# Input statistics of a group normalisation taken in one pass about early group means, with other load sizes and another engine for the first scalings

## The chip, the core and the metric

The kernel runs on one NeuronCore of a Trainium2 chip. The metric is the device time of one execution in microseconds (us). The core has five engines that run their own instruction queues in order: PE (TensorE, matmul), DVE (VectorE), ACT (ScalarE), POOL (GpSimd) and SP (SyncE, which only issues transfers here). Transfers (DMAs) can be issued from the SP, ACT and POOL queues; all of them run on the core's 16 DMA engines.

## The reference, cut to what matters

The input `x` is float32, 384 channels of 192 x 192. Two layers follow each other; the change touches only the first normalisation.

```
x = x + attention(group_norm(x))     # layer 0
x = x + seven_convs(group_norm(x))   # layer 1: 13x13 and six dilated depthwise convolutions

group_norm: 32 groups of 12 channels, mean and variance over 12 x 192 x 192 values
attention:  qkv = W_qkv (1152 x 384) @ x;  2x2 max pooling;  3x3 depthwise convolution;
            8 heads of 48 channels, top-k softmax of q k^T over channels;
            GELU; each cell copied to 2x2; W_proj @ ...
```

The statistics of layer 0 have to be known before any value of `x` can be scaled, and so before the first product of `W_qkv` with scaled values. The whole input (56.6 MB) is therefore read once for the statistics and again, block by block, for the products.

## The kernel before

Channels lie on partitions, in three groups `j` = 0, 1, 2 of 128. The 192 rows are cut into `NB` = 24 blocks of 8 rows (`FB` = 1536 values per channel).

*The statistics stage* is written with an order by hand (`manual_schedule`): instructions stand on each engine in the order of the program text, and each engine works its queue in that order.

- Blocks B = 0 and 1 of all channels (the "rows") are loaded by `load` from SP as four half-blocks of 1,152 KB into the pool `ax`; they stay in memory for the main loop. The other 22 blocks of each `j` (`NX` = 22) are loaded by `load_blocks` one at a time, 768 KB each, in the order of the list `order`: all of j = 0, then 1, then 2 (66 blocks, numbered n). Eight of them (`kept`) stay for early products; the rest go through a ring of eight slots. The issuing queue is ACT for the first eight loads, then POOL for odd n and SP for even n. A slot is loaded again once the engine that read it is done.
- Each block is reduced either by DVE (three `bn_stats` of 512 values, L535) or, for the blocks named in `BY_ACT`, by ACT: two activations that sum (x - pivot) and its square (L531, L532). The pivots are means of what has been read of that channel.
- When a `j` is read, `aggregate` (L501, `bn_aggr`) joins the DVE results into a mean and variance per channel; sums from ACT are turned into the same form by small operations (L522 to L527). 128 channels aren't a whole number of groups of 12, so a few channels of the next `j` are read ahead (`spares`, L550 and L558).
- `group_stats` then joins channels to groups through PE in two passes: weighted means to group means (`mean_of`), group means back to channels, squared differences plus variances to group variances, an inverse square root, and scale and shift back to channels (L113 to L156). It runs for j = 0 (`ga`), j = 1 (`ge`) and j = 2 (`g`), spread between `bn_stats` by generators (`first_chunk`, `early`, `last`).
- Meanwhile PE begins the products that need only j = 0 (`first_chunk`) or j = 0 and 1 (`early`): 18 pieces (`EARLY`), named by block and by one of three output groups. ACT scales an input piece with `ready` (L418), PE multiplies (`multiply`, L429), ACT copies the product out of PSUM to memory (`put_by`, L440) and later back into PSUM (`fill`, L269), so that j = 2 can be added.
- POOL also merges the convolution weights (`merge`), sums 2x2 cells of scaled pieces for later (`sum_one`, L280 to L284) and zeroes buffers for the main loop (L633).

*The main loop* takes the 24 blocks twice, for q and k (12 steps a block) and for v (6 steps a block). A step is six matmul calls (`project`, L671), a 2x2 maximum on DVE (L683), a bias on ACT (L690) and 3x3 taps on DVE (L719). At the first step of block B the two half-blocks of B + 1 are loaded (`load`, L179, into four buffers); ACT scales them from the sixth step on in the first half, and from the third in the second (`normalize`, L651). `input_variance` (L962) works out the input's variance from the stored parts with one small DVE operation per step; it is used in layer 1.

The attention, the projection back (L1459) and layer 1's convolutions (L1371) follow.

Of the kernel before, what the change touches and what calls it, by code (L numbers as in the profile page):

```python
# [58 lines left out]
def tile_attn_then_large_kernel_conv(ctx: ExitStack, tc: tile.TileContext, a: dict, out: bass.AP):  # L59
# [112 lines left out]
    ax = ctx_x.enter_context(tc.tile_pool(name="ax", bufs=4, side="right"))  # L172
    xts = {}


    def load(B, sb):
        row0 = (B % NB * R + sb * SR) * 2
        xt = ax.tile([P, NJ, 2 * SR * W], F32, tag="xt", name=f"xt_{B}_{sb}")
        nc.sync.dma_start(  # L179
            out=xt,  # L180
            in_=x[:, row0 * W : (row0 + 2 * SR) * W].rearrange("(j p) n -> p j n", p=P),
        )
        xts[B, sb] = xt
# [5 lines left out]
    mvx = const.tile([P, 9, 2], F32, name="mvx")  # L189
    BY_ACT = ((4, 7, 10, 13, 16, 19), (4, 5, 7, 12, 15, 18), (0, 1))  # L190
    KINDS = ((0, 2), (0, 1, 2), (0, 2))
    PARTS = []
    terms = []
    for j in range(NJ):
        if j < 2:
            terms.append((len(terms), NJ + j))
        PARTS.append([])
        for q in KINDS[j]:
            share = (0, 1, len(BY_ACT[j]))[q] * R / HS
            if q == 0:  # L200
                share = 1 - (len(KINDS[j]) - 2 + len(BY_ACT[j])) * R / HS
            PARTS[j].append((len(terms), q, share))
            terms.append((len(terms), j))
# [23 lines left out]
    FB = R * 2 * W  # L227
    HB = FB // 2
# [62 lines left out]
    with (  # L291
# [9 lines left out]
        for B in range(2):  # L301
            for sb in range(2):
                load(B, sb)
        FX = NKEEP * FB
        NX = (HW - FX) // FB
        NS0 = 2 * 2 * 2
# [14 lines left out]
        xss, waiting = {}, list(range(NJ * NX))  # L321

        def load_blocks():

            while waiting:
# [9 lines left out]
                eng = nc.scalar if n < 8 else nc.gpsimd if n % 2 == 1 else nc.sync  # L335
                eng.dma_start(out=xs, in_=x[j * P : (j + 1) * P, FX + b * FB : FX + (b + 1) * FB])
# [13 lines left out]
        nc.gpsimd.dma_start(out=gm, in_=a["gm"].rearrange("(j p) g -> p j g", p=P))  # L350
        nc.gpsimd.dma_start(out=gmt[:, :C], in_=a["gmt"])
# [7 lines left out]
        gw = [s1.tile([P, NG], F32, name="gw")]  # L359
# [5 lines left out]
        o = NJ * HS * WS - 2 * SR * WS  # L365
        gw += [free[:, o - n * NG : o - (n - 1) * NG] for n in (1, 2)]
        assert len(gw) == len(terms)

        def merge():

            c0 = BC - 1
            for j in range(NJ):
# [12 lines left out]
                for jj in range(NJ):  # L385
                    for k, _, share in PARTS[jj]:
                        nc.gpsimd.tensor_scalar(gw[k], gm[:, jj], share, None, ALU.mult)
                    yield
                for jj in range(2):
# [4 lines left out]
                    k = P * (jj + 1) - 1  # L394
                    nc.gpsimd.tensor_copy(
                        gmt[:, C + jj * P : C + (jj + 1) * P], gmt[:, k : k + 1].to_broadcast([NG, P])
                    )
# [11 lines left out]
        def rows_stats(n):  # L409
            xt = xts[n // 2, n % 2]  # L410
            for j in range(NJ):
                nc.vector.bn_stats(stats[:, j, 2 * n, :], xt[:, j, :512])
                nc.vector.bn_stats(stats[:, j, 2 * n + 1, :], xt[:, j, 512:])

        def ready(B, sb, j):

            t = xts[B, sb][:, j] if B < NKEEP else kept[j, B - NKEEP][:, :HB]
            nc.scalar.activation(t, t, AF.Identity, bias=gn0[:, j, 1:2], scale=gn0[:, j, 0:1])  # L418
# [23 lines left out]
        def first_chunk():  # L442

            pc = yield from group_stats(s1, s_ps, mvx, "ga", gw, terms[: TWICE[1]], (0,), True)
            yield
            nc.vector.tensor_copy(gn0[:, 0], pc[:, 0])
            yield
            blocks = sorted({B for B, _ in EARLY if B >= NKEEP})
            ready(blocks[0], 0, 0)
# [15 lines left out]
        def early():  # L465
# [5 lines left out]
            for n, (B, m) in enumerate(EARLY):  # L471
# [13 lines left out]
                if n < NKEEP:  # L485
                    ready(n, 1, 1)
# [82 lines left out]
        for _ in range(4):  # L569
            next(last)  # L570
# [1045 lines left out]
```

## Time and profile before

| | us |
|---|---|
| four runs, median | 2866.99 (2863.77 to 2867.78) |
| the profiled execution | 2867.78 |
| its span, first to last instruction | 2866.0 |
| first early product on j = 0 (L429) | 81.48 |
| first early product on j = 1 (L429) | 123.92 |
| first main-loop matmul (L671) | 166.12 |

| engine | busy us | share of the span |
|---|---|---|
| PE | 2740.0 | 96% |
| DVE | 2498.1 | 87% |
| ACT | 1332.6 | 46% |
| POOL | 918.4 | 32% |

Times in a profile line count from the start of the span. In a timeline line they are the start, the duration, the engine, the line of the kernel, the operation, what it writes and reads, the number of instructions, and in brackets the idle time before it and what ended it. In a line of a windows view they are the stretch, its length, the busy time and instruction count of PE, of PE's weight loads, of DVE, ACT and POOL, then PE's granted clock, the DMA engines' share and GB/s. In a line of groups they are line, engine, operation, tiles, shapes and count, then busy us and mean ns of one, then idle time before and its releasers. Matmul ends are modelled, so times on PE are good to some tenths.

### The profile page before, as it was taken

The numbers are of one execution on the slowest core, as the hardware profiler recorded it, in microseconds if no ns is written. First come the engines' busy times: TensorE is split into PE (matmuls) and PEld (weight loads), VectorE is DVE, ScalarE is ACT, GpSimd is POOL, SyncE is SP. The second block draws the span as 40 slices with busy tenths as digits, with TensorE's granted clock in tenths as the row PEclk, the third lists the DMA queues.
The fourth block names the chain that finished last, engine by engine and source line by source line (L and its number), as shares of the span: only waits on it lengthen the run. The fifth ranks groups of instructions, "written<-read, shape, count | busy, mean of one in ns | idle before, by whom it ended". The sixth has DMA issues, their size and how long they took to land.

```text
span 2866.0 us, 37738 instructions
## 1 busy us (share of the span) xinstructions
PE 2740.0 (96%) x13662; PEld 1677.8 (59%) x13662; DVE 2498.1 (87%) x3484; ACT 1332.6 (46%) x2427; POOL 918.4 (32%) x1129
## 2 busy tenths in 40 slices
PE   0699999999999999999999999999999999999998
PEld 0356666666666666666655555545566666666666
DVE  6879997887878888788899988887789999999997
ACT  3755554444445444454444444444334444444443
POOL 4251231332323233231122222232115444445443
PEclk9899999999999999999999999999999999999999
DMA  9941432232423324242332333327889999999996
GB/s 389 419 149 64 134 120 80 86 121 72 135 74 101 102 71 135 67 135 79 102 111 96 113 118 114 118 65 223 233 202 286 261 273 273 271 278 270 256 270 174
DMA packets 269561, 475.75 MB, mean 166 GB/s; under 512 B 25858, under 2 KB 189968, under 8 KB 269248
## 3 DMA queue, kind: packets, MB, share of 16 engines
q1 hardware_dynamic: 204208, 301.51, 37.3%
q0 software_dynamic: 43328, 149.04, 15.6%
q10 hardware_dynamic: 21840, 22.81, 2.3%
q8 instruction: 108, 1.77, 0.3%
q14 instruction: 77, 0.63, 0.1%
HBM read 337.06 MB, written 136.20 MB: 165 GB/s over the span
## 4 chain that ended last, share of the span: by engine, by line
PE 85%; DVE 7%; DMA 5%; ACT 1%; issue 1%; POOL 0%; ACTq 0%; SPq 0%; POOLq 0%; DVEq 0%
PE qkv L671 51%; PE conv L1371 24%; PE pj L1459 4%; DVE v L719 3%; DMA xs<-in_x 3%; PE gram L760 2%; PE tr L748 2%; DVE mx L683 1%; PE av L1131 1%; PE qkv L429 1%; DVE acc L719 1%; DVE stats L535 1%; DMA sm<-sums 1%; DMA v<-in_x 0%; DMA wt<-zd 0%
## 5 line engine op out<-in xcount | busy, mean ns | idle before, releaser
L671 PE MATMUL qkv<-xt,wqk 128*128 128x384 f32 x3304 | 1082.5, 486 | 1.9 <-DVE mx L683 1.1
L671 PEld LDWEIGHTS qkv<-xt,wqk 128*128 128x128 f32 x3304 | 620.1, 190 | 417.0 <-DVE mx L683 4.5
L719 DVE SCALAR_TENSOR_TENSOR acc<-pooled,wd,acc 128x384 f32<-128x384 f32 (+2 forms) x1152 | 733.7, 637 | 30.5
L1371 PE MATMUL conv<-xp,wt 128*64 128x288 f32 (+1 forms) x6016 | 723.9, 404 | 2.6 <-issue 1.9
L1371 PEld LDWEIGHTS conv<-xp,wt 128*64 128x64 f32 x6016 | 463.0, 137 | 260.9 <-issue 2.9
L690 ACT ACTIVATE pooled<-mx,bq 128x192 f32<-128x192 f32 x432 | 196.8, 455 | 900.3 <-DVE mx L683 898.2
L683 DVE TENSOR_REDUCE mx<-qkv 128x192 f32<-128x768 f32 x432 | 412.2, 954 | 200.1 <-PE qkv L671 187.1
L671 PE MATMUL qkv<-xt,wv 128*128 128x384 f32 x1728 | 562.4, 487 | 2.5 <-DVE mx L683 2.2
L671 PEld LDWEIGHTS qkv<-xt,wv 128*128 128x128 f32 x1728 | 326.1, 190 | 233.4 <-DVE mx L683 9.8
L1351 DVE STREAM_TRANSPOSE xp<-xn 128x4608 f32<-128x4608 f32 (+1 forms) x107 | 445.5, 4163 | 15.8 <-PE conv L1371 8.3
L280 POOL TENSOR_TENSOR sum<-xt 128x192 f32<-128x192 f32 x128 | 88.0, 687 | 969.0 <-ACT xt L651 967.9
L719 DVE SCALAR_TENSOR_TENSOR v<-pooled,wd,v 128x384 f32<-128x384 f32 (+2 forms) x576 | 375.4, 652 | 15.2
L1379 ACT ACTIVATE co<-conv,cb 128x288 f32<-128x288 f32 x376 | 186.9, 497 | 380.1 <-PE conv L1371 373.9
L651 ACT ACTIVATE xt<-xt,gn 128x768 f32<-128x768 f32 x278 | 275.5, 1014 | 0.0
L1328 POOL TENSOR_TENSOR raw<-raw,up 128x2496 f32<-128x2496 f32 x46 | 230.0, 5000 | 40.7 <-DMA up<-pd 29.4
L1421 POOL DMA_DIRECT2D out<-o x194 | 107.4, 582 | 371.3 <-DVE o L1412 312.6
L1412 DVE STREAM_TRANSPOSE o<-co 128x2304 f32<-128x2304 f32 (+3 forms) x50 | 211.1, 4223 | 9.7 <-ACT co L1403 8.8
L1459 PE MATMUL pj<-v,wp 128*128 128x384 f32 x432 | 144.7, 493 | 1.3 <-ACT v L1138 0.7
L788 POOL DMA_DIRECT2D zd<-v x96 | 72.0, 756 | 216.1 <-ACT v L779 216.1
L1336 ACT ACTIVATE xn<-raw,par 128x2112 f32<-128x2112 f32 x48 | 103.1, 2149 | 32.1 <-POOL raw L1328 23.3
L1459 PEld LDWEIGHTS pj<-v,wp 128*128 128x128 f32 x432 | 81.7, 192 | 57.6 <-DVE cell L1475 2.3
L281 POOL TENSOR_TENSOR sum<-sum,xt 128x192 f32<-128x192 f32 x128 | 101.0, 789 | 10.8
(296 smaller groups left out, 1919.5 us busy)
## 6 DMA issues: line engine op xcount, KB each, us to landing
xt<-in_x SPq DMA_DIRECT2D x96, 1152.0 KB, 7.4
raw<-in_x SPq DMA_DIRECT2D x182, 312.0 KB, 13.0
out<-o POOLq DMA_DIRECT2D x188, 288.0 KB, 8.3
wt<-zd SPq DMA_DIRECT2D x46, 1024.0 KB, 12.8
zd<-v POOLq DMA_DIRECT2D x96, 416.0 KB, 4.4
up<-pd SPq DMA_DIRECT2D x184, 156.0 KB, 12.5
xs<-in_x POOLq DMA_DIRECT2D x20, 768.0 KB, 10.7
smj<-sums SPq DMA_DIRECT2D x72, 192.0 KB, 2.8
```

What stands on the lines that cost most here:

```text
L651: nc.scalar.activation(xt[:, j], xt[:, j], AF.Identity, bias=gn0[:, j, 1:2], scale=gn0[:, j, 0:1])
L671: nc.tensor.matmul(ps[:, r, : 2 * W], lhsT=wq[:, j, mm * P : (mm + 1) * P], rhs=xt[:, j, r * 2 * W : (r + 1) * 2 * W], start=(j == 0), sto ...
L683: nc.vector.tensor_reduce(mx, ps[:, :, : 2 * W].rearrange("p r (y w x) -> p r w y x", y=2, x=2), AX.XY, ALU.max,)
L690: nc.scalar.activation(pool_t[m][:, k : k + SR, 1 : 1 + WS], mx, AF.Identity, bias=bq[:, m : m + 1])
L719: nc.vector.scalar_tensor_tensor(acc[:, :nt], pool_t[m][:, k0 + dy : k0 + dy + nt, dx : dx + WS], wd[:, m, t : t + 1], acc[:, :nt], ALU.mu ...
L1328: eng.tensor_add(rv, rv, uv.unsqueeze(2).to_broadcast([P, (m1 - m0) * WS, 2]))
L1351: nc.vector.transpose(bass.AP(at.tensor, at.offset, [list(at.ap[0]), [NBQ, n], [1, NBQ], [NQ * NBQ, CC], [ME * NBQ, NE]],), bass.AP(row.te ...
L1371: nc.tensor.matmul(ps[h * MH : (h + 1) * MH, t0:t1], lhsT=wt[:, c, o : o + MH], rhs=d[:, c, g + 2 * t0 : g + 2 * t1 - 1 : 2, :], start=(e ...
L1379: nc.scalar.activation(co[:, c], ps, AF.Identity, bias=cb[:, cc : cc + 1])
L1412: nc.vector.transpose(bass.AP(at.tensor, at.offset, [list(at.ap[0]), [2 * W, n], [BC, NBQ], [W, 2], [1, BC]]), bass.AP(of.tensor, of.offse ...
L1421: engines[u % len(engines)].dma_start(out=bass.AP(out.tensor, out.offset + k * CC * HW + (2 * u + t0 * BR) * W, [[ME * UQ * W, CC * NE], [ ...
L1459: nc.tensor.matmul(ps, lhsT=wp[:, j, i * P : (i + 1) * P], rhs=v[:, j, b * RB : (b + 1) * RB, :].rearrange("p r w -> p (r w)"), start=(j = ...
```

## The change

- The rows are loaded by `load(B, engines)` as six transfers of 768 KB, one per j, from SP, ACT and POOL, 6 KB for each channel and packet instead of 3 KB. In the main loop one transfer of 2,304 KB per block takes the place of two; the pool `ax` has two buffers of a whole block.
- `pivots` takes the rows' statistics at once, ahead of all other blocks, joins them to early group means through PE, and keeps their negatives per channel in `npiv`. The group matrices `gm` and `gmt` are loaded at the start, from ACT.
- `group_scale` takes the place of `group_stats`: all parts are held as difference to the pivot and mean square about it; ACT's sums enter as they are. One accumulation on PE gives both moments of a group. Known terms are accumulated before the last block is done.
- `awake` puts filler matmuls into PE's queue around the chain for j = 1.
- DVE's parts are aggregated in two: up to block `SPLIT` (three before the end for j = 0 and 1, the middle for j = 2) and after it.
- ACT takes three blocks of j = 2 (3, 6 and 10) instead of 0 and 1. `early` yields after its first, second and fourth product, so that these blocks come between.
- `ready` scales on POOL, except for the first piece of each chain, which ACT scales in two halves.
- `load_blocks` issues from SP and POOL, SP for slots that ACT frees and otherwise whichever has issued fewer; the last two blocks of j = 1 and 2 are loaded as two halves of 64 channels from both queues.
- `input_variance` gets four more small operations for each j, over 56 steps instead of 40.

```diff
-    ax = ctx_x.enter_context(tc.tile_pool(name="ax", bufs=4, side="right"))
+    ax = ctx_x.enter_context(tc.tile_pool(name="ax", bufs=2, side="right"))
+    def load(B, engines=None):
+        xt = ax.tile([P, NJ, FB], F32, tag="xt", name=f"xt_{B}")
+        o = B % NB * FB
+        if engines is None:
+            nc.sync.dma_start(out=xt, in_=x[:, o : o + FB].rearrange("(j p) n -> p j n", p=P))
+        else:
+            for j, eng in enumerate(engines):
+                eng.dma_start(out=xt[:, j], in_=x[j * P : (j + 1) * P, o : o + FB])
...
-    BY_ACT = ((4, 7, 10, 13, 16, 19), (4, 5, 7, 12, 15, 18), (0, 1))
+    BY_ACT = ((4, 7, 10, 13, 16, 19), (6, 8, 1, 12, 15, 18), (3, 6, 10))
+    SPLIT = (NX - 3, NX - 3, NX // 2)
...
-        for B in range(2):
-            for sb in range(2):
-                load(B, sb)
+        nc.scalar.dma_start(out=gm, in_=a["gm"].rearrange("(j p) g -> p j g", p=P))
+        nc.scalar.dma_start(out=gmt[:, :C], in_=a["gmt"])
+        for B in range(NKEEP):
+            load(B, (nc.sync, nc.scalar, nc.gpsimd))
...
-                eng = nc.scalar if n < 8 else nc.gpsimd if n % 2 == 1 else nc.sync
-                eng.dma_start(out=xs, in_=x[j * P : (j + 1) * P, FX + b * FB : FX + (b + 1) * FB])
+                src = x[j * P : (j + 1) * P, FX + b * FB : FX + (b + 1) * FB]
+                if j > 0 and n % NX >= NX - 2:
+                    nc.sync.dma_start(out=xs[: P // 2], in_=src[: P // 2])
+                    nc.gpsimd.dma_start(out=xs[P // 2 :], in_=src[P // 2 :])
+                else:
+                    k = int(not free_by_act and issued.get(1, 0) < issued.get(0, 0))
+                    issued[k] = issued.get(k, 0) + 1
+                    (nc.sync, nc.gpsimd)[k].dma_start(out=xs, in_=src)
...
+        def pivots():
+            for B in range(NKEEP):
+                for j in range(NJ):
+                    for q in range(FB // 512):
+                        src = rows_of[B][:, j, q * 512 : (q + 1) * 512]
+                        nc.vector.bn_stats(stats[:, j, B * (FB // 512) + q, :], src)
...
+        def awake(n):
+            ps = s_ps.tile([P, P], F32, tag="awake", name="awake", bufs=1)
+            for _ in range(n):
+                nc.tensor.matmul(ps, lhsT=ident, rhs=ident, start=True, stop=True)
+        def group_scale(name, old, new, out, warm):
...
+            awake(warm[0])
+            add_up_terms(0, len(known))
+            yield
+            for q in sorted({q for _, q in new}):
...
+                nc.vector.tensor_scalar(ds[:, own, 0:1], mvx[:, own, 0:1], npiv[:, q : q + 1], None, ALU.add)
+            nc.vector.tensor_mul(ds[:, own, 1:2], ds[:, own, 0:1], ds[:, own, 0:1])
+            nc.vector.tensor_add(ds[:, own, 1:2], ds[:, own, 1:2], mvx[:, own, 1:2])
+            add_up_terms(len(known), len(both))
+            awake(warm[1])
+            yield
...
+            nc.vector.tensor_copy(d, ps)
+            nc.vector.scalar_tensor_tensor(nve, d[:, 0:1], d[:, 0:1], d[:, 1:2], ALU.mult, ALU.subtract)
+            nc.vector.tensor_scalar(nve, nve, 0.0, -1e-5, ALU.min, ALU.add)
+            nc.scalar.activation(rt, nve, AF.Sqrt, scale=-1.0)
+            nc.vector.tensor_add(m, d[:, 0:1], pg)
+            yield
...
+            nc.tensor.matmul(pc, lhsT=gmt[:, out * P : (out + 1) * P], rhs=sb, start=True, stop=True)
+            awake(warm[2])
+            yield
+            nc.vector.tensor_copy(gn0[:, out], pc)
-        def ready(B, sb, j):
+        def ready(B, sb, j, how="pool"):
             t = xts[B, sb][:, j] if B < NKEEP else kept[j, B - NKEEP][:, :HB]
-            nc.scalar.activation(t, t, AF.Identity, bias=gn0[:, j, 1:2], scale=gn0[:, j, 0:1])
+            if how == "pool":
+                nc.gpsimd.tensor_scalar(t, t, gn0[:, j, 0:1], gn0[:, j, 1:2], ALU.mult, ALU.add)
+            else:
+                for part in range(2):
+                    at = t[:, part * 2 * W : (part + 1) * 2 * W]
+                    nc.scalar.activation(at, at, AF.Identity, bias=gn0[:, j, 1:2], scale=gn0[:, j, 0:1])
...
+            yield from group_scale("ge", [PARTS[0][0][0], PARTS[0][1][0]], new, 1, (12, 6, 4))
+            ready(0, 0, 1, "act")
...
+                if n in (0, 1, 3):
+                    yield False
...
-        for _ in range(4):
-            next(last)
-        next(first)
-        for _ in range(2):
-            next(last)
-        for _ in range(2):
-            next(first)
+        next(last)
+        next(first)
+        next(last)
+        next(first)
+        next(last)
+        next(first)
         whole = multiply(0, NJ, (0,))
-        next(first)
-        pc = in_one(last)
+        assert next(last, last) is last
         multiply(0, NJ, (1,), whole)
...
+                    if q == 2:
+                        m = mvx[:, k]
+                        yield nc.vector.tensor_scalar(m, m, 1.0 / (share * HW), None, ALU.mult)
+                        yield nc.vector.tensor_mul(t, m[:, 0:1], m[:, 0:1])
+                        yield nc.vector.tensor_sub(m[:, 1:2], m[:, 1:2], t)
+                        yield nc.vector.tensor_sub(m[:, 0:1], m[:, 0:1], npiv[:, j : j + 1])
...
                 if u == 0 and 1 <= B < 2 * NB - 1:
-                    for i in range(2):
-                        load(B + 1, i)
+                    load(B + 1)
```

## The prediction

> **What bounds the kernel now.** I read the page first: engine shares and the slices.
>
> ```profile
> span 2866.0 us, 37738 instructions
> PE 2740.0 (96%) x13662; PEld 1677.8 (59%) x13662; DVE 2498.1 (87%) x3484; ACT 1332.6 (46%) x2427; POOL 918.4 (32%) x1129
> PE   0699999999999999999999999999999999999998
> ```
>
> TensorE (PE) is full from the third slice (71.65 us each) to the end. All edits but two (the block loads, the variance) end before the first projection matmul of the main loop (L671), so the change is worth what that start moves. Next, the stretches before it:
>
> ```profile
> 0.00:20.00 20.00, 0.00 (x0) 0.00 (x0) 8.49 (x23) 1.50 (x2) 14.89 (x28) 1.00 0.92 331
> 80.00:100.00 20.00, 17.39 (x44) 8.61 (x44) 14.91 (x26) 16.61 (x20) 1.66 (x3) 1.00 1.02 422
> 140.00:150.00 10.00, 7.57 (x20) 3.20 (x19) 9.64 (x18) 9.76 (x13) 6.16 (x11) 1.00 1.03 409
> 150.00:160.00 10.00, 8.68 (x35) 4.30 (x34) 6.61 (x16) 9.64 (x13) 5.75 (x11) 1.00 0.44 163
> ```
>
> Last columns are clock, DMA share, GB/s: the input streams at some 420 GB/s until about 152 us, and the stage hangs on that. The timeline shows its tail, engine by engine:
>
> ```profile
> 143.57 0.53 POOL L336 DMA_DIRECT2D v<-in_x  x1
> ...
> 152.47 1.87 DVE L535 BATCH_NORM_STATS2 stats<-v 128x6 f32<-128x512 f32 x3
> 154.38 2.00 DVE L501 BATCH_NORM_AGGREGATE mvx<-stats 128x2 f32<-128x408 f32 x1
> ...
> 158.40 0.35 PE L113 MATMUL g_ps<-mvx,stats 128*32 128x1 f32 x6
> 164.42 0.38 PE L156 MATMUL g_pc<-g_sb,gmt 32*128 32x2 f32 x2
> 166.12 15.79 PE L671 MATMUL qkv<-xt,wqk 128*128 128x384 f32 x48
> ```
>
> POOL issues the last input block at 143.57, the DMA view gives it 8.3 us to landing (151.9), VectorE (DVE) starts on it at 152.47, aggregates until 156.38, and the mean and variance go round PE twice between early matmuls. L671 starts 9.7 us after the aggregate. PE is nearly full meanwhile with early products (L429), which a second chain limits: ScalarE (ACT) copies each product out, copies an older one back and scales pieces (L418, 1.02 us).
>
> **The stream's start.** The first 20 us move 331 GB/s against 422: 1.8 MB, or 4.3 us, is all that could be won. The first 2 us (17 GB/s) stay, and so do the small weight loads. Rows in 3 KB packets already ran at 397 and 408 GB/s from 4 to 8 us, so packets twice as long give little. I take 1.5 us; bounds 0 and 3.
>
> **Row statistics and pivots.** Rows cost DVE 12 x 0.680 + 12 x 0.410 = 13.1 us before; 18 full chunks at 0.61 are 11.0. Three small aggregates (0.35 each), a copy, a scale and eight tiny matmuls are added, some 1.6 us. DVE waited 23.5 us for DMA in this stage (11.6 + 7.9 + 4.0), which hides both signs; uncovered they would cancel to 0.5. Block 0 now queues behind all rows on DVE: 9.5 + 11 + 1 is about 21.5 us; the first ring slot it frees comes at some 31 us, where SP and POOL waited until 33 to 34 before. No loss.
>
> **From the second third to the early products.** Before, the aggregate ended at 115.10 and the first early product on j=1 started at 123.92: 8.8 us. After, one pass, priced by the rows of the old chain: 4 DVE operations 0.7, five matmuls 0.5, three DVE 0.55, square root and the statistics chunk put over it 0.75, six DVE 1.1, a matmul 0.55, copy 0.2, half a piece on ACT 0.65 (between 0.455 for 192 elements and 1.014 for 768): 5.0 us. The aggregate ends some 2.6 us sooner (1.5 from the stream, 0.7 as L522 to L527 go, the rest as both queues bring the last two blocks), at 112.5. Early products can start at 117.5, 6.4 sooner.
>
> That isn't all won, since ACT statistics blocks 3, 6 and 10 of the last third (1.56 + 0.19 + 1.48 + 0.19 = 3.4 us each, 10.3 in all) now stand between the first early copies; before, two such blocks were done ahead of the chain. ACT: piece 1.1 and first product 1.3 to 2.6, copy 0.8, then block, copy, block, two copies, block to about 135; fills and copies at 1.63 a product (copies at 142.17 and 143.72, then 145.43, without a scaling between) put the 16th at about 151. On the path only if statistics end sooner.
>
> The clock was 0.50 from 115 to 125 us, and the first early product took 2.96 us to its copy where later ones show 1.56. The filler matmuls can win 1.4 to 2.7 us there; I count none, as ACT's blocks follow. [...]
>
> **Pieces scaled on GpSimd.** Fourteen of the sixteen pieces leave ACT, seven of them in the last third. POOL's rows for such an operation are short (mean ns last before the idle time):
>
> ```profile
> L1328 POOL TENSOR_TENSOR raw<-raw,up 128x2496 f32<-128x2496 f32 x46 | 230.0, 5000 | 40.7 <-DMA up<-pd 29.4 <-DMA raw<-in_x 5.8 <-DMA wt<-zd 3.7
> ...
> L633 POOL MEMSET pooled<- 128x588 f32 x9 | 4.8, 588 | 2.1 <-ACT v L440 2.1
> ...
> L380 POOL TENSOR_SCALAR wb<-wb,bn_r 128x9 f32<-128x9 f32 x9 | 2.9, 320 | 0.2
> L373 POOL TENSOR_SCALAR wf<-wb,bn_r 128x169 f32<-128x169 f32 x3 | 2.2, 729 | 0.2
> ```
>
> The slope between the two TENSOR_SCALAR rows is 2.56 ns an element: 2.3 us for 768; proportion to the longer alone gives 3.3; the long addition runs at 2.0 (1.5 us); the memset's 1.0 is the floor, 0.8. I take 1.9, between slope and long row. Queued behind it on POOL are input loads, which DVE and ACT wait for. In program order three pieces stand between a load whose ring slot comes free at about T+19.5 = 132 us and the last loads; then one load 0.55 and one sum with its store 2.9. The last POOL half-blocks are issued at 132 + 5.7 + 0.55 + 2.9 = 141.1 (before 143.57), and land at 149.4.
>
> [...]
>
> **The tail.** The last two blocks land almost together in halves, so DVE has one left: 149.4 + 1.87 = 151.3. The aggregate covers 11 blocks (198 values): between the rows 54 (0.385) and 408 (1.998) that is 1.04, against 2.00. So 152.3. Then three DVE 0.55, matmuls 0.35, three DVE 0.55, square root 0.25, six DVE 1.1, matmul 0.35: 155.5. Behind it on PE stand the last early product and the whole sixth one, 12 records at 0.3225 (3.87 for 12 in the main loop): 3.9. The first main-loop matmul comes at 159.4 instead of 166.12: 6.7 us sooner.
>
> **Behind the start.** The main loop's first steps keep their order, with POOL's zeroing memsets still gated by the last early copy. Ten sums instead of seven follow them on POOL (3 x 2.7 = 8 us more); nobody waits for these before the second block's buffer is reloaded some 45 us later. Three reductions (0.13) precede DVE's first maximum, which waited 2.77 us. The variance adds 12 tiny DVE operations, about 2 us, one a step; DVE was busy 40.6 of 50 us there with PE full: 0, at most 2. The block load:
>
> ```profile
> xt<-in_x SPq DMA_DIRECT2D x21, 1152.0 KB, 5.4
> ```
>
> That is from 1600 to 1850 us, the tighter phase. The single load starts where the second half did (about 1718.8) and the first scaling of its rows comes at 1735.5: 16.7 us of cover. Twice 5.4 is 10.8; so 0. The cover ends only if a block takes over 16.7; the excess would then hold ACT, 22 times.
>
> **The sum.** The profiled execution took 2867.78 (span 2866.0, 1.8 outside), 0.8 above the median 2866.99. Minus 6.7: 2861.1 for such an execution, 2860.3 as a median. About 0.2% (5.7 us) is what a measurement of this kernel can tell from no change, so my forecast lies just past it.
>
> **Rivals.** *POOL becomes the bound, slower.* Place: the three pieces ahead of the last loads. Each microsecond a piece costs over 1.9 moves the start by 3. At 4.1 the gain is gone; at 6 us the start is 5.6 late: 2872.6. For it: two arithmetic steps on 768 elements are shown by no row, and POOL's queue already let the last load go late (143.57, behind sums). Against: all four rows lie below 3.3. 0.15.
>
> *The early chain ends last.* If ACT's three blocks, or late data for them, hold the early copies by 6 us more than I laid out, the 16th copy is at 157 and the start near 163 to 166: gain 0 to 3, time 2864 to 2867. For: ACT was 96% busy from 140 to 160. Against: the scaling leaves it. 0.18.
>
> *The stream runs clean.* Loads evenly split, rows out of the way, POOL at 0.8 to 1.5 a piece: the last block lands at 147, statistics close behind; start at 155 to 157, gain 9 to 11, time 2856 to 2858. For: 410 to 426 GB/s was held whenever loads were queued. Against: weights and scratch stores still share the end. 0.15.
>
> **How the numbers follow.** Forecast 0.52 (gain 4 to 8.5), rivals 0.15, 0.18 and 0.15. Past 5.7: three fifths of the forecast and the clean stream, and a little besides: 0.50. Within 0.2%: the rest of the forecast and nearly all of the second rival, a third of the first: 0.36. Slower: 0.14, most of the first rival and a late block load. The range takes in the clean stream below with 3 us more, and a POOL piece of 4.5 us above: 2853 to 2869.
>
> **What would show it.** Right: the POOL piece near 1.9 us; first j=1 product near 117; last block landing by 150; an aggregate of about 1.0; one pass of some 3.2 us; first main-loop matmul at 157 to 162 and all later stages shifted alike. Wrong: a piece over 4 us, the first main-loop matmul after 165, main-loop blocks longer than before (50.5 us in the first half, 23.3 in the second).

## The result, and the profile after

| | before | after |
|---|---|---|
| median of the runs (lowest to highest) | 2865.03 (2861.67 to 2888.27), 69 runs | 2875.23 (2864.39 to 2907.12), 44 runs |
| the profiled execution | 2867.78 | 2881.44 |
| first early product on j = 1 | 123.92 | 121.37 |
| first main-loop matmul | 166.12 | 169.75 |
| last main-loop matmul ends | 1904.4 | 1907.6 |
| first matmul of the convolutions | 2112.9 | 2112.7 |
| last matmul of the convolutions ends | 2858.2 | 2871.7 |

The changed kernel is slower: ratio 1.0045, interval 1.0033 to 1.0057. (The ratio isn't the quotient of the two medians.) The forecast of 2860.3 us missed, and the range up to 2869 missed too. Two stages stand out. The statistics end 3.6 us later, where 6.7 us sooner was expected. And the convolutions, whose code the change doesn't touch, take 13.7 us more in the profiled execution, which is itself 6.2 us above the median of after. In between, the late start was gone again by the first matmul of the convolutions. That is one execution of each kernel: over the 19 profiled executions of this document the stretch from the last main-loop matmul to the first of the convolutions took 202.7 to 209.2 us (208.5 in before, 205.1 in after). The spread over the runs is wide as well: the lowest of after is only 2.7 us above the lowest of before, but 34 of its 44 runs lie over 7 us above that, and 9 of the 69 of before over 7 us above theirs.

The page of after:

```profile
span 2879.6 us, 37737 instructions
PE 2749.2 (95%) x13730; PEld 1686.8 (59%) x13730; DVE 2497.9 (87%) x3484; ACT 1312.0 (46%) x2420; POOL 935.9 (33%) x1151
```

The windows view of after, the same stretches as before, and three at the end of the second third (last columns: PE's clock, DMA share, GB/s):

```profile
0.00:20.00 20.00, 0.00 (x0) 0.00 (x0) 3.70 (x13) 1.50 (x2) 10.28 (x18) 1.00 0.93 340
80.00:100.00 20.00, 15.16 (x42) 7.89 (x41) 13.37 (x23) 17.45 (x24) 3.74 (x5) 0.91 1.02 417
...
100.00:105.00 5.00, 3.72 (x47) 3.43 (x45) 4.97 (x11) 4.97 (x7) 1.61 (x3) 1.00 0.99 308
105.00:110.00 5.00, 0.48 (x6) 0.40 (x6) 4.38 (x7) 2.83 (x4) 1.06 (x2) 0.75 1.00 227
110.00:115.00 5.00, 0.00 (x0) 0.00 (x0) 3.79 (x7) 0.00 (x0) 0.03 (x1) 0.50 1.00 343
...
140.00:150.00 10.00, 8.95 (x21) 4.30 (x21) 10.00 (x18) 8.35 (x12) 6.18 (x11) 0.83 1.03 393
150.00:160.00 10.00, 8.48 (x42) 4.12 (x42) 9.07 (x16) 9.34 (x12) 3.78 (x7) 1.00 1.03 296
```

The same three stretches before:

```profile
100.00:105.00 5.00, 3.72 (x7) 2.08 (x8) 4.55 (x9) 3.15 (x6) 0.00 (x0) 0.68 1.02 426
105.00:110.00 5.00, 2.39 (x13) 1.18 (x11) 4.97 (x10) 4.94 (x7) 1.57 (x3) 0.98 0.98 388
110.00:115.00 5.00, 0.27 (x2) 0.18 (x2) 4.83 (x12) 4.97 (x7) 0.00 (x0) 0.70 1.00 406
```

Read share and GB/s together. From 100 to 115 us the 16 DMA engines count as full (0.99 to 1.00), yet they move 227 to 343 GB/s; before had 426, 388 and 406 there at the same share. From 150 to 160 the stream is still running (296 GB/s at 1.03), where before it had drained (163 at 0.44). Both stretches are those in which the last two blocks of a third come in halves of 64 partitions. So a full engine share doesn't tell a full rate here: a share of 1.00 went with 227 GB/s in after, one of 1.02 with 426 in before. The missing bytes from 100 to 115, against the mean of before's three rates (407), are 5 x (99 + 180 + 64) = 1.7 MB, or 4 us of stream.

The timeline's tail of after:

```profile
144.82 1.05 POOL L344 DMA_DIRECT2D v<-in_x  x2
...
156.45 3.66 DVE L618 BATCH_NORM_STATS2 stats<-v 128x6 f32<-128x512 f32 x6 [0.51 <-DMA v<-in_x]
...
160.14 1.05 DVE L595 BATCH_NORM_AGGREGATE mvx<-stats 128x2 f32<-128x198 f32 x1
...
162.31 0.38 PE L468 MATMUL g_ps<-ds,stats 128*32 128x2 f32 x4 [3.43 <-DVE ds L479]
...
165.47 0.38 PE L499 MATMUL g_pc<-g_sb,gmt 32*128 32x2 f32 x2
...
169.75 1.45 PE L760 MATMUL qkv<-xt,wqk 128*128 128x384 f32 x4
```

The DMA view of 140 to 158 us gives the landings of the halves (KB each, median us from issue to landing):

```profile
v<-in_x SPq DMA_DIRECT2D x2, 384.0 KB, 11.4
v<-in_x POOLq DMA_DIRECT2D x2, 384.0 KB, 12.1
```

The last halves leave POOL at 144.82 (forecast 141.1; before 143.57), DVE can begin on the last two blocks at 156.45, and from the aggregate on the chain is as forecast in kind: one pass, 1.05 us for the 198 values, the main loop 8.6 us behind the aggregate.

One line each of the windows view in the convolutions, before and then after:

```profile
2600.00:2800.00 200.00, 200.00 (x1670) 128.04 (x1668) 195.26 (x144) 88.71 (x143) 93.31 (x67) 1.00 1.04 267
```

```profile
2600.00:2800.00 200.00, 193.54 (x1596) 123.12 (x1594) 186.52 (x135) 79.88 (x138) 88.31 (x64) 1.00 1.00 258
```

Before, PE has no gap. After, it misses 6.5 of 200 us. The engines of the transfers are full in both (1.04, 1.00), but move 267 and 258 GB/s. What ended PE's gaps in the whole stage was mostly DVE's weight tile `wt` (4.5 us) and ACT's copies `co` (4.1 us), not a transfer directly; whether the lower rate makes the gaps or follows from them isn't shown.

### The profile page after: what moved, and what is told of

Same layout as the page of the kernel before. It is cut to its first block, busy times and chain, and to the rows that moved or that the text cites. A ratio compares the mean times of both kernels' runs of the same rounds, so it can differ in the third digit from the quotient of the medians.

```text
span 2879.6 us, 37737 instructions
## 1 busy us (share of the span) xinstructions
PE 2749.2 (95%) x13730; PEld 1686.8 (59%) x13730; DVE 2497.9 (87%) x3484; ACT 1312.0 (46%) x2420; POOL 935.9 (33%) x1151
## 4 chain that ended last, share of the span: by engine, by line
PE 74%; DMA 11%; DVE 8%; ACT 3%; POOL 2%; issue 1%; SPq 1%; ACTq 0%; POOLq 0%; DVEq 0%
PE qkv L760 51%; PE conv L1465 14%; DMA up<-pd 4%; DVE v L808 3%; PE pj L1553 3%; DMA wt<-zd 2%; PE gram L849 2%; PE tr L837 2%; DVE mx L772 1%; POOL raw L1422 1%; DMA raw<-in_x 1%; PE av L1225 1%; DMA xs<-in_x 1%; ACT xn L1430 1%; DVE stats L618 1%
## 5 line engine op out<-in xcount | busy, mean ns | idle before, releaser
L1473 ACT ACTIVATE co<-conv,cb 128x288 f32<-128x288 f32 x376 | 179.1, 493 | 253.9 <-PE conv L1465 174.4
L877 POOL DMA_DIRECT2D zd<-v x96 | 72.0, 757 | 208.5 <-ACT v L868 208.5
L1412 DVE SCALAR_TENSOR_TENSOR wt<-mask,sdb,wt 128x64 f32<-128x64 f32 x384 | 81.2, 287 | 28.1 <-DMA wt<-zd 28.1
```

Of the source, the lines that this page charges most:

```text
L1473: nc.scalar.activation(co[:, c], ps, AF.Identity, bias=cb[:, cc : cc + 1])
```

## The experiments

What differs in the convolutions, if not the code, is the place of the tiles: the new tile `npiv` (20 bytes) takes 32 bytes of the constant pool, and by the two programs' allocations the tiles allocated after it from the left-hand end of SBUF begin 32 bytes further on (`v` at byte 20320 of a partition instead of 20288). Of the convolutions' buffers, both of `o` (results) and two of three each of `raw` (input) and `wt` (weights) began at a multiple of 64 bytes before, none after. So there are two theories: the addresses (A), with the rivals that work left behind by the new order of the statistics stage is the cause (B) or chance between executions (E); and the halves (C, or C1 if they also bring the convolutions' loss), with the rival that something else cuts the rate (D). All runs, in five groups that ran on one chip each (e1 to e4, e5 to e8, e9 to e12, e13 to e16, e17):

| run | median (lowest) | before beside it | ratio, interval | first main-loop matmul |
|---|---|---|---|---|
| e1 before, +32 bytes | 2870.74 (2865.52) | 2864.74 | 1.0025, 1.0013 to 1.0038 | 167.8 |
| e2 before, +64 bytes | 2867.82 (2864.56) | 2864.74 | 1.0014, 0.9999 to 1.0029 | 166.5 |
| e3 after, packed | 2872.12 (2863.34) | 2864.74 | 1.0028, 1.0011 to 1.0045 | 173.2 |
| e4 packed, whole blocks | 2860.21 (2857.47) | 2864.74 | 0.9981, 0.9971 to 0.9991 | 161.8 |
| e5 after, whole blocks | 2866.96 (2863.31) | 2865.92 | 0.9995, 0.9976 to 1.0015 | 165.5 |
| e6 packed, halves by columns | 2862.20 (2858.76) | 2865.92 | 0.9991, 0.9970 to 1.0011 | 164.9 |
| e7 before, halves | 2877.62 (2872.08) | 2865.92 | 1.0029, 1.0014 to 1.0044 | 176.1 |
| e8 as e4, no fillers | 2862.80 (2858.81) | 2865.92 | 0.9990, 0.9970 to 1.0010 | 163.7 |
| e9 as e4, right-hand end moved | 2861.09 (2858.05) | 2866.38 | 0.9989, 0.9976 to 1.0002 | 165.7 |
| e10 before, right-hand end moved | 2868.31 (2863.13) | 2866.38 | 1.0004, 0.9992 to 1.0015 | 165.2 |
| e11 before, +96 bytes | 2869.67 (2867.37) | 2866.38 | 1.0025, 1.0002 to 1.0048 | 167.0 |
| e12 before, +128 bytes | 2867.74 (2865.13) | 2866.38 | 1.0009, 0.9996 to 1.0022 | 167.6 |
| e13 as e4, pieces on ACT | 2864.25 (2862.08) | 2866.04 | 0.9991, 0.9975 to 1.0007 | 167.8 |
| e14 as e4, late start | 2870.22 (2867.89) | 2866.04 | 1.0008, 0.9992 to 1.0024 | 170.4 |
| e15 as e3 again | 2867.35 (2864.35) | 2866.04 | 1.0006, 0.9986 to 1.0027 | 167.8 |
| e16 as e4 again | 2862.21 (2857.57) | 2866.04 | 0.9983, 0.9963 to 1.0003 | 164.5 |
| e17 packed, cut at 32 and 96 | 2865.81 (2861.81) | 2867.00 | 0.9993, 0.9966 to 1.0020 | 168.1 |

The last column is of one execution each. It varies by some 2 us among before and its shifted copies (e1, e2 and e10 to e12: 165.2 to 167.8), and by 2.7 and 5.4 us between two executions of one program (e4 and e16, e3 and e15).

### Halves or whole blocks

**e3: the new tile packed.**

```
-    shift = const.tile([P, NJ], F32, name="shift")
+    shift8 = const.tile([P, 2 * NJ + 2], F32, name="shift")
+    shift = shift8[:, :NJ]
-    npiv = const.tile([P, NJ + 2], F32, name="npiv")
+    npiv = shift8[:, NJ:]
```

> The changed kernel with its new tile npiv put into the unused rest of the 32 bytes that the tile shift occupies, so that v and every tile of the convolution stage has exactly the address that it has in the kernel before; no instruction differs. Theory A: the convolution stage is gapless again; what stays is the start of the main loop at 169.8 instead of 166.1, of which most was taken back by the start of the convolution: 2865 to 2869. Rival B: no change from the changed kernel, 2875. A third outcome, that the statistics stage moves too (half of its ring lies in v, whose address shifts by 32), would show in a first main-loop matmul away from 169.8.

Measured 7.4 us over the before beside it, where after is 10.2 over its own, with the convolutions' addresses those of before. The runs are spread: 2863 to 2866 five times, 2879 to 2888 five times. Theory A alone doesn't carry the loss.

**e4, and e16 again: whole last blocks too.**

```
-                if j > 0 and n % NX >= NX - 2:
+                if False:
```

> As the run before (npiv packed), and the last two blocks of the second and third thirds are loaded whole, 128 partitions by one transfer on SP or GpSimd by turns, instead of as two halves of 64 partitions each on both queues. Theory C (the 64-partition halves cut what the sixteen DMA engines move while they are full: 227 to 308 GB/s at 100 to 110 us where before had 388 to 426): 400 GB/s or more from 100 to 115 and up to the end of the stream, the last block lands some 5 to 7 us sooner, first main-loop matmul at 162 to 165, and 4 to 7 us less than the run before: 2859 to 2864. Rival D (the throughput falls for another reason, such as the scratch stores and the sums that share the queues): first main-loop matmul at 169 to 170 as in the changed kernel, no change against the run before.

> The packed kernel with whole blocks again (2860.2, ratio 0.9981, 1 of 11 runs over 7 us above the lowest), for a larger sample and on the same chip as the three others: faster than before by 3.5 to 5.5 us, and 1 or 2 of 12 runs over 7 us above the lowest. If its low share of long runs was chance: 3 to 5 of 12.

The windows view of e4, and its timeline's tail:

```profile
100.00:105.00 5.00, 3.84 (x46) 3.50 (x44) 4.93 (x12) 4.94 (x9) 0.53 (x1) 1.00 1.00 410
105.00:110.00 5.00, 0.60 (x8) 0.42 (x8) 4.04 (x6) 3.17 (x5) 1.05 (x2) 0.84 1.03 426
110.00:115.00 5.00, 1.05 (x9) 1.03 (x10) 4.22 (x14) 0.00 (x0) 0.53 (x1) 0.50 1.01 418
145.00:150.00 5.00, 4.65 (x14) 2.04 (x13) 5.00 (x9) 4.84 (x7) 1.82 (x4) 1.00 1.02 406
```

```profile
138.57 0.54 POOL L349 DMA_DIRECT2D v<-in_x  x1 [0.23 <-issue]
...
152.54 1.05 DVE L596 BATCH_NORM_AGGREGATE mvx<-stats 128x2 f32<-128x198 f32 x1
...
157.52 0.38 PE L500 MATMUL g_pc<-g_sb,gmt 32*128 32x2 f32 x2 [1.45 <-DVE g_sb L498]
...
161.80 4.68 PE L761 MATMUL qkv<-xt,wqk 128*128 128x384 f32 x14
```

At the same share the rate is 406 to 426 GB/s. The last block is issued 6.3 us sooner than in after, the aggregate comes 7.6 us sooner, the main loop 8.0 us. The medians of both samples lie under before, by 4.5 and 3.8 us; the interval of e16 just reaches 1 (1.0003). On one chip the halves cost 2872.12 - 2860.21 = 11.9 us (e3 and e4) and 2867.35 - 2862.21 = 5.1 us (e15 and e16) by the medians, 5.9 and 6.8 us by the lowest runs. Theory C holds; the size of the medians varies with the convolutions, of which more below.

The DMA view of e4 from 138 to 160 us gives the last block, whole, a landing time too:

```profile
v<-in_x POOLq DMA_DIRECT2D x1, 768.0 KB, 11.5
```

So a last block takes over 8.3 us here even when it is whole. What the halves lower is the rate of the stream, in both thirds (e3 had 304, 247 and 388 GB/s from 100 to 115 us and 272 from 145 to 150; e4 410, 426, 418 and 406), and with it the time at which the last loads are issued.

**e5: the halves alone undone**, `npiv` where the change put it.

> The changed kernel with one thing undone: the last two blocks of the second and third thirds come whole, 128 partitions in one transfer, on SP or GpSimd by turns; npiv stays where it is, so that the later tiles lie 32 bytes further on than in the kernel before. Theory C (halves cost the statistics stage its lead): first main-loop matmul at 161 to 164, as with the packed tile (161.8), against 169.8. For the convolution two theories part here. C1 (the halves also brought the convolution's loss): gapless convolution, 2859 to 2862. A (addresses add a loss of their own): the start as early, but 5 to 8 us lost in the convolution, 2865 to 2870.

1.0 us over the before beside it (0.3 under it without its longest run, 2908.62), where e4 was 4.5 under: the addresses would cost 4 to 6 us, in the sense of A. But these are two chips, the intervals overlap (0.9976 to 1.0015, e4 0.9971 to 0.9991), and the profiled start of 165.5 is past the 161 to 164 expected. Its rate from 100 to 115 us is 413, 417 and 418 GB/s. Against after (10.2 us over its before, ratio 1.0045) this one condition takes 9.2 us off, and with them the loss: the ratio is 0.9995.

**e6: two transfers per block, cut by columns.**

```
-                    nc.sync.dma_start(out=xs[: P // 2], in_=src[: P // 2])
-                    nc.gpsimd.dma_start(out=xs[P // 2 :], in_=src[P // 2 :])
+                    nc.sync.dma_start(out=xs[:, : FB // 2], in_=src[:, : FB // 2])
+                    nc.gpsimd.dma_start(out=xs[:, FB // 2 :], in_=src[:, FB // 2 :])
```

> npiv packed, and the last two blocks of the second and third thirds in two transfers again, but cut by columns: 128 partitions by 768 elements (3 KB a partition) on each of SP and GpSimd. If the number of partitions is what cuts the throughput (theory C): 400 GB/s or more from 100 to 115 and from 145 to the end, first main-loop matmul at 160 to 163, 2858 to 2862. If it is that two queues carry one block, or that the issues are doubled (rival): 230 to 310 GB/s in these stretches again, first main-loop matmul after 168, 2866 to 2875.

The windows view of e6:

```profile
105.00:110.00 5.00, 0.47 (x6) 0.38 (x6) 5.00 (x9) 2.16 (x4) 0.53 (x1) 0.73 1.01 413
...
145.00:150.00 5.00, 4.64 (x13) 2.03 (x12) 5.00 (x10) 4.82 (x7) 1.95 (x4) 1.00 1.03 407
```

Same sizes, same two queues, same number of issues, full rate. Only from 100 to 105 it was 313, and there the share was 0.86. So it isn't the split, the queues or the issues; it is the cut through the partitions: from 105 to 110 and from 145 to 150 us 413 and 407 GB/s with columns, 247 and 272 with halves (e3). The start of 164.9 is 1.9 us past the expected stretch, the time 0.2 us.

**e7: the halves put into the kernel before.**

```
-                eng.dma_start(out=xs, in_=x[j * P : (j + 1) * P, FX + b * FB : FX + (b + 1) * FB])
+                src = x[j * P : (j + 1) * P, FX + b * FB : FX + (b + 1) * FB]
+                if j > 0 and n % NX >= NX - 2:
+                    nc.sync.dma_start(out=xs[: P // 2], in_=src[: P // 2])
+                    nc.gpsimd.dma_start(out=xs[P // 2 :], in_=src[P // 2 :])
+                else:
+                    eng.dma_start(out=xs, in_=src)
```

> The kernel before with the halves alone: the last two blocks of the second and third thirds as 64 partitions on SP and 64 on GpSimd each; nothing else changed. Theory C: throughput falls below 310 GB/s around 105 and at the end of the stream, the last block lands 4 to 7 us later, first main-loop matmul at 170 to 173 instead of 166.1, and the time is 4 to 7 us longer if nothing further happens, 2869 to 2872; with C1 (the halves bring a loss in the convolution too) 2872 to 2880. Rival D (the halves cost nothing here): within 0.2% of 2865.

The windows view of e7:

```profile
100.00:105.00 5.00, 3.30 (x7) 1.83 (x8) 4.32 (x9) 3.53 (x6) 1.04 (x2) 0.76 0.93 290
105.00:110.00 5.00, 2.81 (x13) 1.37 (x11) 4.97 (x10) 4.94 (x7) 1.60 (x3) 0.90 1.02 275
...
145.00:150.00 5.00, 3.73 (x10) 1.83 (x11) 2.93 (x5) 4.85 (x7) 3.30 (x6) 1.00 1.02 237
```

The main loop starts 10 us later (176.1) and the median is 11.7 us higher (ratio 1.0029): more than expected. In the profiled execution (2875.10 us, before 2867.78) 7.2 of the 10 us are left at the first matmul of the convolutions, and these took 745.4 us from first to last matmul, as before (745.3). So the halves alone don't have to lengthen the convolutions, and C1 has no support here.

**e17: transfers as small, cut elsewhere.** SP loads partitions 32 to 95 and POOL 0 to 31 and 96 to 127.

> The packed kernel, its four last blocks cut by partitions again, but at other places: partitions 32 to 95 in one transfer on SP, 0 to 31 and 96 to 127 in two on GpSimd. The transfers are as small as the halves. [...] Fewer partitions than 128 in a transfer as such, wherever they lie (rival): 230 to 310 GB/s again, first main-loop matmul at 168 to 173.

From 105 to 110 us it moved 269 GB/s, from 145 to 150 390, from 150 to 155 264. The 390 says little, since the rate falls only at 149 us (414 GB/s up to there, 244 from 149 to 154); the other two lie within the expected 230 to 310. The SP part landed in 5.0 and 6.8 us at the end of the second third, against 6.9 and 9.9 in e3, and the start (168.1) is near e15's (167.8). The interval of its time (0.9966 to 1.0020) overlaps those of e15 and e16. Whether the place of the partitions counts or their number in one transfer stays undecided.

### Addresses

**e1, e2, e11, e12: before with 32, 64, 96 and 128 bytes more ahead of its tiles** (4, 8, 12 or 16 in place of the first number):

```
-    gn0 = const.tile([P, NJ, 2], F32, name="gn0")
+    gn0 = const.tile([P, NJ + 4, 2], F32, name="gn0")[:, :NJ]
```

> The kernel before, with one constant tile (gn0) made 32 bytes longer, so that every tile allocated after it starts 32 bytes further on in SBUF, where the changed kernel has them (v at byte 20320 instead of 20288); no instruction differs. Theory A (address: what the changed kernel loses in the convolution is the 32-byte shift of the tiles that its transfers read and write): the convolution stage loses its gapless PE, with idle time on PE released by DMA, and the run takes about 8 to 10 us more than before, 2873 to 2875. Rival B (order: the loss comes from work that the changed statistics stage leaves behind, such as sums and variance): no change, 2865 within 0.2%.

> The kernel before with the same constant tile made 64 bytes longer: everything lies 64 bytes further on, again a multiple of 64. Theory A in its narrow form (what matters is the start address modulo 64): no change against before, 2865 within 0.2%. Rival A2 (any shift disturbs, for instance through the distance of tiles that share something): slower by 8 us or so, like the 32-byte shift. Rival B: no change either.

> The kernel before with the constant tile 96 bytes longer: the start addresses modulo 64 are those of the 32-byte shift again. Theory A: like the 32-byte shift, 3 to 6 us longer than before, 2869 to 2872, and a lowest run above 2864.5. Rival E: 2865 to 2868, with a lowest run near 2862.

> The kernel before with the constant tile 128 bytes longer: start addresses modulo 64 and modulo 128 are those of the kernel before. Theory A: no change, 2865 with a lowest run near 2862. Theory A2 (what counts is another distance, since the 64-byte shift gave 2867.8 with a lowest run of 2864.6): longer by 2 to 6 us. Rival E: within 0.1% of before, with some long runs.

Medians over the before beside them: +6.0, +3.1, +3.3, +1.4. The lowest runs: +3.1, +2.1, +3.5, +1.3. The two odd multiples of 32 are slower with intervals above 1; for the two even ones the intervals hold 1. So a shift by 32 or 96 bytes, with no instruction changed, cost 3 to 6 us. That the even multiples cost nothing is not shown: all four medians and all four lowest runs lie above those of before, and on each chip the intervals of the odd and the even shift overlap. The narrow rule (start modulo 64) is not proven.

Nor do the traces show where the time goes. These are the last 200 us of the convolutions in e11 (96 bytes) and in e2 (64 bytes):

```profile
2600.00:2800.00 200.00, 200.00 (x1670) 128.17 (x1668) 195.04 (x144) 87.82 (x143) 93.51 (x66) 1.00 1.03 272
```

```profile
2600.00:2800.00 200.00, 192.59 (x1588) 120.35 (x1584) 184.19 (x133) 78.06 (x134) 91.05 (x61) 1.00 1.03 259
```

e11, with the odd shift, has no gap on PE; e2, with the even one, has, and its execution (2891.12) was a long one. From first to last matmul the convolutions took 749.5 us in e1 and 746.8 in e11, 747.1 in e12 and 745.3 before.

**e9 and e10: the buffers at the right-hand end of SBUF moved to multiples of 64 too**, in e4 and in before:

```
+    padr = ctx.enter_context(tc.tile_pool(name="padr", bufs=1, side="right"))
+    padr.tile([P, 8], F32, name="padr")
```

> The packed kernel with whole blocks (2860.2), and one unused tile of 32 bytes allocated first from the right-hand end of SBUF, so that the tiles allocated from there start 32 bytes lower: the third buffers of raw and wt, the second of up, xn and xp, and the row blocks xt now start at multiples of 64 bytes too. Theory A (a start at an odd multiple of 32 bytes makes the loads of the convolution dearer): their transfers get shorter by some per cent, the lead of the feeding chain grows faster than before, fewer long runs; median 2856 to 2860, and highest run below 2870. Rival E (the loss in the convolution is a matter of chance between executions, not of addresses): median 2860 to 2863 and single runs to 2870 to 2890 as in the other kernels.

> The kernel before with the same unused 32-byte tile at the right-hand end, all buffers of the convolution at multiples of 64 bytes. Theory A: convolution at least as short as before (745 us from first to last matmul), single long runs rarer, median 2862 to 2865. Rival E: no change, 2865 with single long runs.

Nothing gained: e9 5.3 us under its before, like e4 and e16, with runs up to 2875; e10 1.9 over it with an interval around 1. Theory A in the form "each buffer off a multiple of 64 costs" has no support here; what counts among the moved tiles was not isolated.

### Chain, pieces, late start

**e8: no fillers** (`awake` called with 0, 0, 0 in `ge`).

> As the packed kernel with whole blocks (2860.2, first main-loop matmul at 161.8), without the 22 filler matmuls around the second scale's chain (awake with 0, 0 and 0 instead of 12, 6 and 4). If the fillers stand in the way of the small matmuls (in the changed kernel 12 of them ran from 116.35 to 119.28 at half the clock ahead of the chain's matmuls): first early product on the second third some 2 us sooner, and 0 to 2 us less in all, since the stream sets the end: 2858 to 2860. If they keep the clock up: first product as late or later, main-loop start up to 2 us later, 2860 to 2862. Both lie within 0.2%, so the trace decides, not the time.

The first product on j = 1, e4 and then e8:

```profile
119.17 5.33 PE L524 MATMUL qkv<-xt,wqk 128*128 128x384 f32 x16
```

```profile
117.39 7.03 PE L524 MATMUL qkv<-xt,wqk 128*128 128x384 f32 x16 [0.99 <-ACT xt L513]
```

From the end of the aggregate (113.12 and 112.21) to the first product it is 6.05 us with fillers and 5.18 without: they stand in the chain for 0.9 us. The 16 records then take 5.33 instead of 7.03 us; the mean clock from 115 to 120 us was 0.63 against 0.50. The first copy comes 7.5 and 8.1 us after the aggregate. Two small effects of opposite sign; the times don't tell them apart.

**e13: the pieces back on ACT.**

```
-                nc.gpsimd.tensor_scalar(t, t, gn0[:, j, 0:1], gn0[:, j, 1:2], ALU.mult, ALU.add)
+                nc.scalar.activation(t, t, AF.Identity, bias=gn0[:, j, 1:2], scale=gn0[:, j, 0:1])
```

> The packed kernel with whole blocks, and the fourteen pieces that GpSimd scales put back on ScalarE (one instruction of 768 elements each, 1.01 us). Prediction's view: ACT's copies of the early products end later by the seven pieces of the last third, 7 x 1.0, of which up to three stand behind waits for data; main-loop start 3 to 6 us later than 161.8, 2862 to 2866. Rival: the stream and DVE's statistics set the start, and ACT's extra work lies beside them: start within 1 us, 2860 to 2861.

2.0 us over e16 on the same chip, start 167.8 against 164.5. By the medians the move to GpSimd is worth about 2 us, though the intervals overlap.

**e14: 30 fillers ahead of the last early product.**

```
         assert next(last, last) is last
+        awake(30)
```

> The packed kernel with whole blocks, and 30 filler matmuls put on PE ahead of the last early product, some 8 to 12 us, so that the main loop starts at about 170 to 173, as in the packed kernel with halves, though its blocks were loaded whole. F (a later start of the main loop alone brings the long convolutions): the lowest run 2864 to 2868, and about half of the runs 8 to 25 us above it, as with the halves. G (it does not; the halves act in another way or the long runs are not tied to the edit): lowest run 2864 to 2868, and no more than 2 or 3 of 12 runs over 8 us above it.

> The changed kernel with npiv packed and halves as they are (2872.1 on another chip, where 6 of 12 runs lay over 7 us above the lowest, 2863.3), on the same chip as the run with whole blocks below and the late start above. F and C1 (with halves, long convolutions are the rule): again about half of the runs over 7 us above the lowest. G (chance): a share as low as in the run with whole blocks.

e14 started at 170.4 and gave 8.0 us more than e16; one of its 12 runs lay over 7 us above its lowest, and PE is busy for all 200 us from 2600 to 2800. F, that a late start alone brings the long convolutions, falls. The halves of e15, on the same chip, had 3 of 12 such runs, where e3 had 6; e16 1 of 12, e4 1 of 11, but e6, e8 and e9 5, 4 and 4 of 12, and before beside them 14 of 140; e1 had 5 of 12, after itself 34 of 44. Long runs occur in every kernel; they are commoner in after than in before, but which edit brings that, 12 runs a kernel don't settle. Three that were profiled had their time in the convolutions: 769.4 us in e2, 759.0 in after, 758.5 in e3, whose tiles there lie where before has them. A fourth didn't: e9's, 8.5 us above its lowest run, had 744.0 us. The line of e3:

```profile
2600.00:2800.00 200.00, 193.91 (x1601) 123.28 (x1598) 186.27 (x138) 82.34 (x141) 86.61 (x62) 1.00 1.06 259
```

Like after's: transfers full, fewer GB/s, PE short by 6. So this gap needs no shifted address. What makes an execution long stays open.

## Why the prediction was wrong, point by point

**The tail, first failing step.** The prediction let the two halves of the last block land together at 149.4, 8.3 us after their issue, the time a whole block took on one queue. Measured: issued at 144.82, median landing 12.1 us for POOL's halves and 11.4 for SP's, so about 156.9, and DVE began on the last two blocks at 156.45. Already the second third's halves had cost some 4 us of stream; with whole blocks (e4) the last issue came 6.3 us sooner. The mistake was to price a transfer of 64 partitions by bytes, although no row of before showed one: the stream then moved 227 to 308 GB/s instead of 406 to 426 (e4). What in such a transfer lowers the rate, the place of its partitions or their number, e17 didn't decide.

In e4 the last block, whole, landed at 150.1, close to the 149.4. That is partly luck: it was issued 2.5 us before the forecast 141.1 and took 3.2 us longer than 8.3.

**Behind the start, second failing step.** "All later stages shifted alike" was argued from instructions and queues. It had no term for what the convolutions, with full transfers (a DMA share of 1.04 before) and PE just without a gap (200.00 of 200 us), make of a change elsewhere; the profiled execution of after lost 13.7 us there. It also left out that a new constant tile moves the later tiles by 32 bytes, and such a shift alone cost 3 to 6 us (e1, e11). That this cost lies in the convolutions is argued, not shown (e11, e2, e3), and why after has so many long runs stays open. Nor did the start carry through: of 3.6 us at the first main-loop matmul nothing was left at the first matmul of the convolutions (2112.7 against 2112.9), in a stretch that varies by over 6 us between executions.

**The sum without these two.** With both taken out (e4, e9, e16) the gain is 3.8 to 5.3 us, against 6.7 in the sum. The steps can be checked in e4. Aggregate on j = 1 done at 113.1 (forecast 112.5); the 16th early copy at 151.13 (151); last aggregate done at 153.6 (152.3); scale and shift on PE at 157.9 (155.5), since the one pass takes 4.3 us, not 3.2; then the 3.9 us of early products, 161.8 (159.4). An estimate for after from medians on several chips: -4.5 on average, halves +5.1 to +11.9, shift +3.3 to +6.0, together +4 to +13; measured +10.2. So wide a sum fits easily and proves little.

**The stream's start** was sized at 1.5 us. The first 20 us moved 340 GB/s instead of 331, which is 0.18 MB or 0.4 us. The lower bound, 0, was nearer.

**Pieces on GpSimd.** The term was over-sized, in the change's disfavour. The groups of after:

```profile
L508 POOL TENSOR_SCALAR v<-v,gn 128x768 f32<-128x768 f32 x7 | 6.8, 976 | 3.3 <-DVE gn L502 3.2
```

0.976 us instead of 1.9, near the 0.8 estimated from the memset's row (588 ns for 588 elements). The slope between the rows of 9 and 169 elements does not carry on: from 169 elements (0.729 us) to 768 only 0.25 us is added. The first rival falls with it; the loss came from elsewhere.

**The early chain** (second rival) happened in part: in after ACT waited 2.85 us for a late block at 135.60, and the 16th copy came at 158.13 instead of 151. But the late loads made both late, not ACT's three blocks; in e4, with the same three blocks, the 16th copy was on time.

**Fillers, block load, variance: right.** Counted at nothing, the fillers gave no time that the runs resolve (e8). The main loop, with single block loads and the variance in its steps, took 1737.8 us against 1738.3, from its first matmul to its last.

**What should have shown it.** The prediction's own test, "wrong: the first main-loop matmul after 165", came true. The other loss breaks "all later stages shifted alike", but no rival had a place for it.

## What to carry to other kernels

Cut a transfer by columns, not through the partitions, when two queues shall share it; with 64 partitions on each of two queues the stream moved 227 to 308 GB/s, with whole blocks 406 to 426 (e4), with blocks cut by columns 413 and 407 (e6). Look at GB/s beside the DMA share, as a full share hid the slow transfers here (1.00 at 227 GB/s in after). Before saying that a distant stage shifts alike, compare the start addresses of its tiles in both programs: moving tiles by 32 or 96 bytes cost 3 to 6 us with no instruction changed (e1, e11), for a reason that stays open. Look at all runs and not at one profile when a stage has no slack. The version with both mended lies below both kernels: 0.9981 of before (0.9971 to 0.9991, e4), and 0.9983 (0.9963 to 1.0003, e16).

## What the runs showed of the hardware that was not expected

- 16 DMA engines counted as full (0.99 and 1.00) while the stream with half-partition loads ran at 308 and 227 GB/s (after, 100 to 110 us); with the same bytes cut by columns it ran at 413 (e6, 105 to 110 us).
- Moving the tiles behind one constant by 32 or 96 bytes, no instruction changed: 1.0025 of before in both cases, with intervals above 1; by 64 or 128 bytes 1.0014 and 1.0009, with 1 inside the interval.
- One and the same program took up to 24 us more in one execution than in another (e3: 2863.34 to 2887.87). Profiled long executions had the DMA engines full at 258 or 259 GB/s and gaps on PE; e13, at 261 GB/s, had none.
- One-input arithmetic with two steps on 768 elements a partition took GpSimd 0.976 us.
